# One read-back of the table's rows for both outer blocks, and block 0's norm first on VectorE

## The chip, the cores and the metric

The kernel runs on 1 core of one Trainium2 chip. The metric is device time in microseconds for one execution; lower is better. In the profile PE is TensorE (PEld its weight loads), DVE is VectorE, ACT is ScalarE, POOL is GpSimd, SP is SyncE, which issues the plain DMAs.

## The reference: one graph layer with four relations

There are 625 nodes with 512 features and 20,625 weighted edges of four types (10,000 in both directions and one loop per node), sorted by destination. Each node sums the messages of its edges, is normalized, and goes through a feed-forward network:

```python
h = maximum(layernorm(x), 0)
xs = h[src]
for r in range(4):
    w_r = where(edge_type == r, edge_weight, 0)
    total_msg += (xs @ W_rel[r] + b_rel[r]) * w_r[:, None]
agg = segment_sum(total_msg, dst) / maximum(segment_sum(edge_weight, dst), 1)[:, None]
x1 = layer_norm(h + h @ W_self + b_self + agg, ln1_g, ln1_b)
ffn = gelu(x1 @ W_ffn1 + b_ffn1) @ W_ffn2 + b_ffn2
out = x + layer_norm(x1 + ffn, ln2_g, ln2_b)
```

## The kernel before: a table of messages, then sums by block

The 625 nodes lie in five blocks of 128 rows. The kernel has two parts.

*The rows.* TensorE computes h @ W_rel[r] for each relation and block (`table_rows`, L403): 20 chunks of 128 rows with 512 floats. Each is scaled and biased on VectorE (L416) and stored to a table in device memory by SP (L418). Chunks 15 to 19 stay on the chip in tiles of their own (`m`), and chunks 9 to 14 stay in the three buffers `tr` that hold two chunks each (`held`). Chunks 0 to 8 are only in device memory.

*The sums.* Two ways are in use. For blocks 0 and 4 (`OUTER`), most of the edges whose destinations lie in that one block are put into a matrix of weights from all 2560 table rows to the block's 128 nodes (`sums_w`; block 0's is read from device memory, block 4's is read and then added to by the products of L613 with copies on VectorE and ScalarE, L556 to L566). A sum is then 20 products, one for each chunk (`chunk_sum`, L1302). All other edges go by gathers: GpSimd fetches 128 table rows with one indirect DMA (`gather`, L1159), 99 times, and six more for edges at the start of the inner blocks (`gather_first`, L1216), into ten buffers `ms` in turn. A unit of three gathers is added up: the first scaled on ScalarE (`first_row`, L1165), the others added on VectorE (`row_added`, L1183), then for most units split in a high and a low part (L1169 on ScalarE, L1173 on VectorE), and one or two products on TensorE bring it to the nodes (`edge_sum`, L1205 to L1208). A buffer `ms` comes free when its row has been used.

Each block's sums are added into `z` (`accumulate`, L429, which takes the block's own product, `self_part`, L441, too). Then comes the first norm (`first_norm`: statistics L880, mean L331, root steps L862 to L869, centred L887, scaled L892, bias L896), the turn of its rows by TensorE (L351) with a copy by ScalarE (L1363), the feed-forward (up L928, gelu L932, down L946), the second norm (sum L956, statistics L959, centred L966, scaled L971) and the store by SP (L997). The blocks go through the feed-forward in the order 0, 4, 1, 2, 3. Block 3 is the last, and its norm takes a power on GpSimd (L344) for the root steps.

*What sets the order.* The instructions of the second part are put in order by a planner (`Plan`). Each operation is named with its engine, an estimated duration, what it comes after, the buffers that it takes and gives back, and a rank; `level` replaces the first number of the rank. The planner runs through time and lets each engine take the ready operation with the lowest key. The result is a fixed order for each engine. On the chip an engine waits at an instruction that is not ready, with all that stand behind it. `LAND` and `LATE` are the planner's estimates for the landing of a gather.

Before the change, block 0's sum takes the resident chunks first and then chunks 0 to 8, for which SP reads the table back (`chunk_load`, L1297, five loads, each as soon as one of the three buffers `tr` is free). Block 4's sum follows and starts with chunks 0 to 14, all read back again (eight loads). Both use one accumulator (`one`), so block 4's sum starts when block 0's is in `z`.

## Time and profile before

| what | value |
|---|---|
| median of 3 runs | 260.74 us (260.15 to 263.15) |
| the profiled execution, its time | 262.26 us |
| its span, first to last instruction | 260.5 us |
| mean granted TensorE clock | 0.993 |
| busy: PE, PEld, DVE, ACT, POOL | 246.4, 141.4, 200.5, 74.8, 172.0 us |
| loads of the table by SP (L1297) | 13: 11 of 512 KB, 2 of 256 KB |
| gathers (L1159, L1216) | 99 and 6 |

A row of a timeline gives start, length, engine, line, operation, and in brackets how long the engine had been idle before it and what ended that. A row can merge several instructions (xN). A 128x512 product in f32 shows as two entries. Busy time is what the engine spent in instructions; it doesn't tell whether the end depended on them. TensorE's lengths overlap, as products are pipelined: the distance from one start to the next is the pace.

### The profile page before, as it was taken

The page shows a single profiled execution, that of the slowest core. Times are in us where ns is not written, and L with a number is a line of the kernel's source. Part 1 is how long each engine was busy: PE and PEld are TensorE (multiplying, and loading weights), DVE is VectorE, ACT ScalarE, POOL GpSimd, SP SyncE. Part 2 cuts the span into 40 slices and gives each one's busy share as a digit, 9 for nine tenths or more (in the row PEclk, how much of TensorE's full clock was granted, in tenths as well). Part 3 has the DMA queues.
Part 4 walks back from the last instruction along what each step waited for, and adds up shares of the span by engine and source line. Part 5 has one row for each costly group of instructions (what it writes and reads, how often), then busy time and mean ns, then how long its engine had stood idle before and what let it go on. Part 6 is the DMA issues. An engine that isn't in the chain of part 4 may idle for free. (4 is left out here: it accounts for less than half of the span.)

```text
span 260.5 us, 3515 instructions
## 1 busy us (share of the span) xinstructions
PE 246.4 (95%) x1051; PEld 141.4 (54%) x1051; DVE 200.5 (77%) x503; ACT 74.8 (29%) x224; POOL 172.0 (66%) x230
## 2 busy tenths in 40 slices
PE   8899999999999969999959999989999998899996
PEld 6444444445445625443424444864685964675964
DVE  2896999997979964839879399997798985973614
ACT  3017300000031573623121142641223632310420
POOL 4478889887888577777778777777777777100000
PEclk9999999999999999999999999999999999799999
DMA  5999999972272599799997977777776677330101
GB/s 191 361 402 416 379 382 360 321 285 81 73 253 85 199 363 328 227 346 299 367 325 219 374 232 201 218 191 208 213 212 205 199 204 213 111 110 6 44 0 44
DMA packets 24055, 60.20 MB, mean 231 GB/s; under 512 B 4401, under 2 KB 8753, under 8 KB 22882
## 3 DMA queue, kind: packets, MB, share of 16 engines
q0 software_dynamic: 9936, 27.58, 35.0%
q1 hardware_dynamic: 13808, 30.94, 32.1%
q10 hardware_dynamic: 290, 1.44, 1.6%
q8 instruction: 9, 0.15, 0.2%
q14 instruction: 12, 0.10, 0.1%
HBM read 50.77 MB, written 9.17 MB: 230 GB/s over the span
## 5 line engine op out<-in xcount | busy, mean ns | idle before, releaser
L1159 POOL DMA_INDIRECT ms<-table,row_i x99 | 97.2, 982 | 30.8 <-issue 13.4
L403 PE MATMUL ps<-wr,hT 128*128 128x512 f32 (+2 forms) x168 | 71.2, 576 | 0.0
L686 POOL DMA_INDIRECT cells<-weight,cell x45 | 48.6, 1080 | 9.0 <-issue 6.4
L403 PEld LDWEIGHTS ps<-wr,hT 128*128 128x128 f32 x168 | 30.6, 190 | 33.8 <-issue 29.9
L1183 DVE SCALAR_TENSOR_TENSOR add<-ms,wgt_g,add 128x512 f32<-128x512 f32 x48 | 35.7, 748 | 16.8 <-DMA ms<-table,row_i 14.9
L928 PEld LDWEIGHTS ps<-x1T,w_sb 128*128 128x128 f32 x320 | 39.1, 197 | 5.2 <-issue 3.2
L928 PE MATMUL ps<-x1T,w_sb 128*128 128x128 f32 (+1 forms) x320 | 39.7, 281 | 0.9 <-ACT gT L932 0.9
L1165 ACT ACTIVATE add<-ms,ed 128x512 f32<-128x512 f32 x30 | 20.7, 692 | 66.5 <-DMA ms<-table,row_i 47.3
L946 PE MATMUL ps<-w_sb,gT 128*128 128x512 f32 (+3 forms) x96 | 36.2, 522 | 0.0
L1302 PE MATMUL acc<-tr,sums_w 128*128 128x512 f32 x60 | 27.7, 595 | 0.0
L599 ACT ACTIVATE ohw<-os,w 128x128 fp32r<-128x128 f32 x36 | 11.4, 389 | 56.3 <-DVE os L581 55.3
L946 PEld LDWEIGHTS ps<-w_sb,gT 128*128 128x128 f32 (+1 forms) x96 | 16.6, 188 | 14.4 <-issue 11.8
L932 ACT ACTIVATE gT<-ps,bf 128x128 f32<-128x128 f32 (+1 forms) x40 | 13.3, 362 | 19.6 <-PE ps L928 14.9
L441 PE MATMUL ps<-ws_sb,hT 128*128 128x512 f32 x40 | 18.3, 592 | 0.0
L1302 PEld LDWEIGHTS acc<-tr,sums_w 128*128 128x128 f32 x60 | 11.0, 190 | 12.3 <-issue 11.2
L1208 PE MATMUL acc<-es,oh 128*128 128x512 f32 x24 | 12.9, 626 | 3.2 <-DVE es L1183 3.2
L416 DVE SCALAR_TENSOR_TENSOR tr<-ps,rx,brel_bc 128x512 f32<-128x512 f32 x15 | 11.2, 744 | 3.3 <-POOL idle L689 2.1
L1173 DVE TENSOR_TENSOR el<-add,eh 128x512 fp32r<-128x512 f32 x18 | 12.3, 681 | 0.9 <-ACT eh L1169 0.8
L1169 ACT CAST eh<-add 128x512 fp32r<-128x512 f32 x18 | 10.5, 581 | 8.2 <-DVE add L1183 8.2
L956 DVE TENSOR_TENSOR ow<-ps,z 128x512 f32<-128x512 f32 (+3 forms) x6 | 3.6, 599 | 11.4 <-PE ps L946 11.3
L441 PEld LDWEIGHTS ps<-ws_sb,hT 128*128 128x128 f32 x40 | 7.6, 190 | 8.7 <-issue 8.6
L1205 PE MATMUL acc<-eh,oh 128*128 128x512 f32 x18 | 11.7, 651 | 0.0
(215 smaller groups left out, 302.5 us busy)
## 6 DMA issues: line engine op xcount, KB each, us to landing
tr<-table SPq DMA_DIRECT2D x11, 512.0 KB, 6.3
w_sb<-in_L_gnn_W_ffn_dram SPq DMA_DIRECT2D x2, 2048.0 KB, 9.5
table<-tr SPq DMA_DIRECT2D x15, 256.0 KB, 6.3
wr<-in_L_gnn_W_rel_dram SPq DMA_DIRECT2D x3, 1024.0 KB, 8.8
cells<-zeros SPq DMA_DIRECT2D x2, 1280.0 KB, 12.5
ms<-table,row_i POOLq DMA_INDIRECT x99, 3.8
rows<-in_rows_dram SPq DMA_DIRECT2D x1, 1536.0 KB, 13.0
sums_w<-cells ACTq DMA_DIRECT2D x1, 1280.0 KB, 5.9
```

Source lines behind the costliest of these rows:

```text
L403: nc.tensor.matmul(p_[:, :h.stop - h.start], hT[i][:, k, :], wr_sb[r][:, k, h], start=(k == 0), stop=(k == KD - 1))
L441: nc.tensor.matmul(p[0], hT[i][:, k, :], ws_sb[:, k, :], start=(k == 0), stop=(k == KD - 1))
L686: s = nc.gpsimd.indirect_dma_start(out=cells[i][:, :], out_offset=bass.IndirectOffsetOnAxis(ap=cell[i][:, k:k + 1], axis=0), in_=weight[i] ...
L928: nc.tensor.matmul(pu[:, :nn], w1_sb[:, k, f * P:(f + 1) * P], x1T_b()[:, k, :nn], start=(k == 0), stop=(k == KD - 1))
L932: nc.scalar.activation(box["gT"][:, f, :nn], pus[f][:, :nn], AF.Gelu, bias=bf1[:, f:f + 1])
L946: nc.tensor.matmul(po[h][:n, :w], box["gT"][:, f, at], w2_sb[:, f, c], start=(f == 0), stop=(f == KF - 1))
L1159: nc.gpsimd.indirect_dma_start(out=ms[j], out_offset=None, in_=table[:, :], in_offset=bass.IndirectOffsetOnAxis(ap=row_i[:, j:j + 1], axis=0))
L1165: nc.scalar.activation(box["sum"], ms[j], AF.Copy, scale=wgt[:, j:j + 1])
L1173: nc.vector.tensor_sub(box["low"], box["sum"], box["high"].bitcast(F32))
L1183: nc.vector.scalar_tensor_tensor(to, ms[j], wgt_g[:, k, q - 1:q], box["sum"], op0=ALU.mult, op1=ALU.add)
L1208: nc.tensor.matmul(acc[bs], ohs[0][:, q, :].bitcast(F32), box["sum"] if "sum" in box else ms[j], start=(k == 0), stop=last)
L1302: nc.tensor.matmul(acc[b,], sums_w[b][:, c, :], kept[(b, c) if (b, c) in kept else c], start=first, stop=last)
```

## The change: one load for both blocks, and other ranks

Both outer blocks now use the same copy of a chunk. `turns` gives the order of the 40 products: block 0's resident chunks, then block 4's sum with chunks 9 to 14, then for each load of chunks 0 to 8 block 0's products and block 4's, then block 4's with chunks 15 to 19. A buffer `tr` is given back by block 4's product, as that is the second to use it. So there are five loads instead of thirteen, and the first waits until block 4's weights are complete (`banked`). As both sums are open at once, block 4's has one of the four general accumulators (`ps`) instead of `one`. The own products of blocks 0 and 4 get `level` 1.4, which puts them ahead of the chunk products (1.5). Block 0's addition to `z` and its first norm without the bias get `level` -1, ahead of all else on VectorE. The planner's estimates for a gather's landing are changed. No computation is added or left out.

```diff
@@ -410,7 +410,7 @@
                 kept["pair"] = const.tile([P, CH, D], F32, tag="tr", name=f"tr_{c}", bufs=LA)
             m = kept["pair"][:, k, :]
             if c in held:
-                kept[OUTER[0], c] = m
+                kept[c] = m
         row0 = r * NP + i * P
         for p_, h in zip(p, at):
             made_row.append(nc.vector.scalar_tensor_tensor(m[:, h], p_[:, :h.stop - h.start], rx[:, i, 1:2],
@@ -1008,12 +1008,12 @@
     SUM = 3
     WARM = 24
     ES = 7
-    LAND, LATE = 3.6, ((8, 2.0), (40, 1.2))
+    LAND, LATE = 3.6, ((8, 2.5), (40, 0.5))
     HOTS_AT, SELF_AT, ADDS_AT = (15, 16, 17), 15, (16, 17, 18)
     OHS = 3
     OW = 5
     GT = 2
-    GATHER = 1.26
+    GATHER, LOADED = 1.26, 6.2
     SLACK = 1.2
     LATER = 0.3
     PARTED = 1, 1
@@ -1146,8 +1146,9 @@
     for n, b in enumerate((OUTER[0], OUTER[1], *inner)):
         first, second, added = self_part(b)
         rank = (2, 0.1 * n) if n < len(OUTER) else (5, n)
-        s0 = op("PE", 1.735, first, take=["ps"], rank=rank)
-        s = op("PE", 1.735, second, after=[s0], give=["T"], lag=0.25, rank=rank)
+        level = 1.4 if n < len(OUTER) else None
+        s0 = op("PE", 1.735, first, take=["ps"], rank=rank, level=level)
+        s = op("PE", 1.735, second, after=[s0], give=["T"], lag=0.25, rank=rank, level=level)
         own[b] = op("DVE", 0.68, added, after=[s], give=[("ps", s0)], rank=(0.6,) if b in OUTER else None, level=4.5)
 
     acc = {}
@@ -1291,15 +1292,15 @@
                    after=[m, first_ready], give=["acc"] if b == bs[-1] else [], rank=(0.3, n), level=1.5 if len(bs) == 1 else 0.05)
             adds[b].append(m)
 
-    def chunk_load(b, c, n):
-        t = const.tile([P, CH, D], F32, tag="tr", name=f"tr_{b}_{c}", bufs=LA)
-        kept.update({(b, c + k): t[:, k, :] for k in range(n)})
+    def chunk_load(c, n):
+        t = const.tile([P, CH, D], F32, tag="tr", name=f"tr_again_{c}", bufs=LA)
+        kept.update({c + k: t[:, k, :] for k in range(n)})
         nc.sync.dma_start(t[:, :n, :], table[c * P:(c + n) * P, :].rearrange("(k p) d -> p k d", p=P))
 
     def chunk_sum(b, c, first, last):
         if first:
-            acc[b,] = ps_one.tile([P, D], F32, tag="one", name=f"acc{b}")
-        nc.tensor.matmul(acc[b,], sums_w[b][:, c, :], kept[(b, c) if (b, c) in kept else c], start=first, stop=last)
+            acc[b,] = ps_one.tile([P, D], F32, tag="one", name=f"acc{b}") if b == OUTER[0] else buffer("ps")
+        nc.tensor.matmul(acc[b,], sums_w[b][:, c, :], kept[c], start=first, stop=last)
 
     landed = op("cells", CELLS, None)
     banked, before_ = [op("SP", 0.3, lambda: load_sums(1), after=[landed], lag=6.5, rank=(0, -1))], None
@@ -1331,19 +1332,22 @@
                        after=[before_, *banked[-1:]], rank=(0.5, i), level=0.25)
                 banked.append(op("ACT", 1.05, lambda steps=steps: steps["c"](), after=[e], give=[("ps", bank_op)], rank=(2, i), level=4.5))
 
-    m, ld, t, here = {b: None for b in OUTER}, None, None, {}
+    m, ld, t, here, first_of = {b: None for b in OUTER}, None, None, {}, {}
     stay = range(NL, NC)
-    for i, (b, c) in enumerate([(OUTER[0], c) for c in (NC - 2, *held, *stay[:-2], NC - 1, *range(held[0]))]
-                               + [(OUTER[1], c) for c in (*range(NL), *stay)]):
-        if (b, c) not in here and c < NL and (b, c) not in kept:
+    loaded = [range(c, min(c + CH - (c + NL) % CH, held[0])) for c in range(held[0]) if c == 0 or (c + NL) % CH == 0]
+    turns = [(OUTER[0], c) for c in (NC - 2, *held, *stay[:-2], NC - 1)] + [(OUTER[1], c) for c in held] \
+        + [(b, c) for some in loaded for b in OUTER for c in some] + [(OUTER[1], c) for c in stay]
+    for i, (b, c) in enumerate(turns):
+        if c < held[0] and c not in here:
             n = CH - (c + NL) % CH
-            ld = op("SP", 0.3, lambda b=b, c=c, n=n: chunk_load(b, c, n), after=[ld], take=["tr"], lag=6.2, order=True,
-                    rank=(0, i))
-            here.update({(b, c + k): ld for k in range(n)})
-        first, last = m[b] is None, i % NC == NC - 1
+            ld = op("SP", 0.3, lambda c=c, n=n: chunk_load(c, n), after=[ld], take=["tr"], lag=LOADED, order=True, rank=(0, i))
+            here.update({c + k: ld for k in range(n)})
+        first, last = m[b] is None, (b, c) == [t_ for t_ in turns if t_[0] == b][-1]
         m[b] = op("PE", 0.87, lambda b=b, c=c, first=first, last=last: chunk_sum(b, c, first, last),
-                  after=[m[b], here.get((b, c)), *(banked if b == OUTER[1] else [])], take=["one"] if first else [],
-                  give=["tr"] if c < NL and (c + NL) % CH == CH - 1 else [], lag=0.25, rank=(2, 2 + 0.01 * i), level=1.5)
+                  after=[m[b], here.get(c), *(banked if b == OUTER[1] else [])],
+                  take=[("one", "ps")[OUTER.index(b)]] if first else [],
+                  give=["tr"] if c < NL and b == OUTER[1] and (c + NL) % CH == CH - 1 else [], lag=0.25, rank=(2, 2 + 0.01 * i), level=1.5)
+        first_of.setdefault(b, m[b])
         if i == 8:
             t = op("PE", 0.2, lambda: at_.update(copied=total_outside()), after=[m[b], first_ready], take=["ps"], lag=8.0, rank=(2, 2.085))
             t = op("DVE", 0.15, lambda: at_["copied"](), after=[t], give=[("ps", t)], lag=2.0, rank=(0.5,), level=4.5)
@@ -1351,7 +1355,8 @@
             op("PE", 0.1, read_outside, after=[t, m[b]], rank=(2, 2.365))
     for b in OUTER:
         adds[b].append(op("DVE", 0.72, lambda b=b: add_to(b, lambda: acc[b,], slice(0, P)),
-                          after=[m[b], first_ready], give=["one"], rank=(0.4,)))
+                          after=[m[b], first_ready], give=["one" if b == OUTER[0] else ("ps", first_of[b])], rank=(0.4,),
+                          level=-1 if b == OUTER[0] else None))
 
     turned = {}
     sums_done = {}
@@ -1371,7 +1376,8 @@
             made[name] = op(eng, us, fn, after=[made[a] for a in needs] if needs else dep + [own[b]],
                             lag=1.0 if name == "x1" and b != inner[-1] else 0.08, take=["ow"] if name in ("a", "x1") else [],
                             give=[("ow", made["a"])] if name == "x1" else [],
-                            rank=(0.4,) if b in OUTER and name != "bias" else None)
+                            rank=(0.4,) if b in OUTER and name != "bias" else None,
+                            level=-1 if b == OUTER[0] and name != "bias" else None)
         p = {}
         parts_ = ((0, KD // 2), (KD // 2, KD)) if b == inner[-1] else ((0, KD),)
         for k0, k1 in parts_:
```

SP, behind the loads of weights and the table's stores (`tr_4_9` is block 4's own read of chunks 9 and 10, `tr_again_1` the common read of chunks 1 and 2); the numbers at the ends of names count tiles:

```order
-L1297 DMA tr_4_9_1315<-table_152 128x2x512
-L1297 DMA tr_4_11_1322<-table_152 128x2x512
-L1297 DMA tr_4_13_1330<-table_152 128x2x512
+L706 DMA sums_w4_980<-cells_4_100 128x2560
+L1298 DMA tr_again_0_1201<-table_152 128x512
+L1298 DMA tr_again_1_1211<-table_152 128x2x512
+L1298 DMA tr_again_3_1229<-table_152 128x2x512
+L1298 DMA tr_again_5_1262<-table_152 128x2x512
+L1298 DMA tr_again_7_1277<-table_152 128x2x512
 L1143 TENSOR_LOAD n_out_157
```

Ten of the thirteen old loads stand above this piece; block 4's weights (L706) are read ahead of all loads in both orders.

TensorE at the last sums of gathered rows (L1208 before, L1209 now; `es_124` is the last unit of three, the next row a single gather), with block 2's feed-forward around them and block 3's turn (L351). Before:

```order
L1208 MATMUL acc3_1_1701<-es_124_1891,oh_122_1844 128x512
L1208 MATMUL acc3_1_1701<-ms_8_951,oh_125_1874 128x512
L928 MATMUL ps_1_79<-x1T_2_1752,w1_sb_93 128x128 x4
L928 MATMUL ps_0_78<-x1T_2_1752,w1_sb_93 128x128 x4
L928 MATMUL ps_3_81<-x1T_2_1752,w1_sb_93 128x128 x4
L946 MATMUL ps_2_80<-w2_sb_94,gT_2_1855 128x512 x4
L351 MATMUL ps_1_79<-ident_120,ow_0_953 128x128 x2
L351 MATMUL ps_0_78<-ident_120,ow_0_953 128x128 x2
L946 MATMUL ps_2_80<-w2_sb_94,gT_2_1855 128x512 x4
L928 MATMUL ps_3_81<-x1T_3_1955,w1_sb_93 128x128 x4
```

Now:

```order
L1209 MATMUL acc3_1_1675<-es_124_1871,oh_122_1824 128x512
L1209 MATMUL acc3_1_1675<-ms_3_946,oh_125_1853 128x512
L928 MATMUL ps_1_79<-x1T_2_1775,w1_sb_93 128x128 x4
L928 MATMUL ps_0_78<-x1T_2_1775,w1_sb_93 128x128 x4
L946 MATMUL ps_3_81<-w2_sb_94,gT_2_1826 128x512 x6
L351 MATMUL ps_2_80<-ident_120,ow_0_953 128x128 x2
L351 MATMUL ps_1_79<-ident_120,ow_0_953 128x128 x2
L946 MATMUL ps_3_81<-w2_sb_94,gT_2_1826 128x512 x2
L928 MATMUL ps_0_78<-x1T_3_1938,w1_sb_93 128x128 x4
```

Behind the last sum there are two up-projections instead of three, and behind the turn two down products instead of four; three up-projections stand between the unit before and this one in both orders.

VectorE on the way to block 3's norm (`acc3_1` is its last sum, L880 the statistics, L966 and L971 the second norms of blocks 0, 4 and 1). Before:

```order
L966 SCALAR_TENSOR_TENSOR ow_1_954<-ow_4_957,mv_y1_0_1887,rows_89 128x512
L868 SCALAR_TENSOR_TENSOR rs_y1_0_1889<-rs_y1_0_1889 128x1
L869 SCALAR_TENSOR_TENSOR rs_y1_0_1889<-rs_y1_0_1889 128x1
L971 SCALAR_TENSOR_TENSOR ow_0_953<-ow_2_955,rs_y4_0_1791,xs_87 128x512
L868 SCALAR_TENSOR_TENSOR rs_y1_0_1889<-rs_y1_0_1889 128x1
L869 SCALAR_TENSOR_TENSOR rs_y1_0_1889<-rs_y1_0_1889 128x1
L429 SCALAR_TENSOR_TENSOR z_145<-acc3_1_1701,rdeg_179,z_145 128x512
L971 SCALAR_TENSOR_TENSOR ow_4_957<-ow_1_954,rs_y1_0_1889,xs_87 128x512
L880 BN_STATS st_z3_1932<-z_145 128x6
```

Now:

```order
L971 SCALAR_TENSOR_TENSOR ow_2_955<-ow_1_954,rs_y0_0_1652,xs_87 128x512
L971 SCALAR_TENSOR_TENSOR ow_0_953<-ow_3_956,rs_y4_0_1793,xs_87 128x512
L429 SCALAR_TENSOR_TENSOR z_145<-acc3_1_1675,rdeg_179,z_145 128x512
L966 SCALAR_TENSOR_TENSOR ow_2_955<-ow_4_957,mv_y1_0_1863,rows_89 128x512
L880 BN_STATS st_z3_1914<-z_145 128x6
L971 SCALAR_TENSOR_TENSOR ow_4_957<-ow_2_955,rs_y1_0_1865,xs_87 128x512
L331 BN_AGGR mv_z3_1921<-st_z3_1914 128x2
L334 TENSOR_SCALAR rs_z3_1923<-mv_z3_1921 128x1
L887 SCALAR_TENSOR_TENSOR ow_1_954<-z_145,mv_z3_1921,rows_89 128x512
```

The addition of the last sum (L429) now stands ahead of block 1's centring (L966), which writes the buffer that block 0's output is stored from, and the scaled outputs of blocks 0 and 4 stand right ahead of it.

Block 0's addition and norm, which stood among the row additions of units 50 to 58, now stand among those of units 65 to 75, directly behind block 0's last chunk product.

## The prediction

> **What bounds the kernel now.** I read the table of groups first, then GpSimd's rows in order of time, the waits of TensorE from the end of the rows on, the busy time of four stretches, and last the timeline of TensorE and VectorE over the last 40 us.
>
> GpSimd in order of time (start, length, idle before), the first two gathers, one in the middle, the last two; above them the two groups that count them (count, sum, mean ns):
>
> ```profile
> L1159 POOL DMA_INDIRECT ms<-table,row_i x99 | 97.2, 982 | 30.8 <-issue 13.4
> L1216 POOL DMA_INDIRECT ms<-table,x_row x6 | 5.7, 945 | 1.8 <-DMA ms<-table,row_i 0.9 <-issue 0.6 <-DVE rs_z L868 0.3
> ...
> 88.09 1.10 POOL L1159 DMA_INDIRECT ms<-table,row_i  x1 [0.94 <-DVE od L591]
> 89.50 1.01 POOL L1159 DMA_INDIRECT ms<-table,row_i  x1 [0.30 <-issue]
> ...
> 136.39 2.37 POOL L1159 DMA_INDIRECT ms<-table,row_i  x1 [0.30 <-DVE z L429]
> ...
> 220.47 0.94 POOL L1159 DMA_INDIRECT ms<-table,row_i  x1 [0.30 <-issue]
> 221.72 0.94 POOL L1159 DMA_INDIRECT ms<-table,row_i  x1 [0.30 <-DVE add L1183]
> ```
>
> 105 gathers stand in 134.6 us, 1.28 us each: 0.95 of issue and 0.30 of fixed gap. The gap stays 0.30 where a releaser is named, so no gather ever waits for a buffer. From 88 to 222.7 us GpSimd's issuing sets the pace. One issue took 2.37 us, 1.42 more than the usual 0.95.
>
> Busy time by stretch (length, then PE, PEld, DVE, ACT, POOL, clock, DMA share, GB/s), and the two large waits of TensorE before 220 us (start, length, idle before):
>
> ```profile
> 88.00:142.00 54.00, 48.43 (x146) 22.93 (x145) 39.14 (x89) 21.57 (x47) 41.42 (x42) 1.00 0.91 311
> 142.00:153.00 11.00, 11.00 (x27) 4.93 (x26) 6.43 (x10) 1.90 (x3) 8.26 (x10) 1.00 0.93 329
> 153.00:182.00 29.00, 27.39 (x122) 17.38 (x121) 27.20 (x59) 11.73 (x23) 22.28 (x23) 1.00 0.72 204
> 182.00:222.00 40.00, 38.30 (x203) 26.40 (x201) 32.58 (x74) 14.78 (x33) 30.27 (x32) 1.00 0.72 208
> 222.00:227.10 5.10, 4.66 (x18) 3.61 (x19) 4.93 (x13) 1.60 (x4) 0.66 (x1) 0.67 0.40 116
> ...
> 94.57 1.10 PE L1208 MATMUL acc<-ms,oh 128*128 128x512 f32 x2 [1.82 <-issue]
> ...
> 136.73 1.12 PE L1208 MATMUL acc<-es,oh 128*128 128x512 f32 x2 [3.03 <-DVE es L1183]
> ```
>
> TensorE is almost full too, but its large waits stand before sums of gathered rows (L1208 takes them, or what VectorE made of them; the third, 1.74 us, is in the next fence). DMA is at 0.91 to 0.93 while the table is read back and at 0.72 with gathers alone.
>
> TensorE at the end (start, length; a 128x128 or 128x512 f32 product is two of its entries):
>
> ```profile
> 222.28 0.49 PE L1206 MATMUL acc<-el,oh 128*128 128x512 f32 x1 [1.74 <-DVE el L1173]
> 222.93 1.52 PE L1208 MATMUL acc<-es,oh 128*128 128x512 f32 x2 [0.16 <-DVE es L1183]
> 224.24 4.13 PE L928 MATMUL ps<-x1T,w_sb 128*128 128x128 f32 x24
> ...
> 229.07 1.02 PE L1208 MATMUL acc<-ms,oh 128*128 128x512 f32 x2
> 229.93 2.84 PE L928 MATMUL ps<-x1T,w_sb 128*128 128x128 f32 x24
> 232.61 3.60 PE L946 MATMUL ps<-w_sb,gT 128*128 128x512 f32 x8
> 236.05 0.60 PE L351 MATMUL ps<-ident,ow 128*128 128x128 f32 x4
> 236.48 3.60 PE L946 MATMUL ps<-w_sb,gT 128*128 128x512 f32 x8
> 239.92 7.31 PE L928 MATMUL ps<-x1T,w_sb 128*128 128x128 f32 x64
> 247.06 7.11 PE L946 MATMUL ps<-w_sb,gT 128*128 128x384 f32 x32
> ```
>
> After the last sum (229.07) block 2's feed-forward fills TensorE; at 236.05 block 3's normalized rows are turned; four more products of block 2 (236.48 to 239.92) stand ahead of block 3's feed-forward, which then runs to 254. VectorE on the same stretch:
>
> ```profile
> 220.87 0.75 DVE L1183 SCALAR_TENSOR_TENSOR add<-ms,wgt_g,add 128x512 f32<-128x512 f32 x1 [2.47 <-DMA ms<-table,row_i]
> 225.71 0.74 DVE L1183 SCALAR_TENSOR_TENSOR es<-ms,wgt_g,add 128x512 f32<-128x512 f32 x1
> 229.50 0.75 DVE L966 SCALAR_TENSOR_TENSOR ow<-ow,mv_y,rows 128x512 f32<-128x512 f32 x1 [1.82 <-DMA out_dram<-ow]
> 231.48 0.74 DVE L429 SCALAR_TENSOR_TENSOR z<-acc,rdeg,z 128x512 f32<-128x512 f32 x1
> 235.02 0.88 DVE L892 SCALAR_TENSOR_TENSOR ow<-ow,rs_z,rows 128x256 f32<-128x256 f32 x2 [0.47 <-POOL rs_z L344]
> ```
>
> The turn at 236.05 follows VectorE's last step of the norm (235.02 to 235.90), whose chain started at 231.48. So the end is: gathers (GpSimd), then VectorE's chain to the turn, then TensorE's filler, then 14.1 us of TensorE and the last norm and store.
>
> **The change part by part.**
>
> *The eight loads that go.* Issues to landing, from the table of DMA issues:
>
> ```profile
> tr<-table SPq DMA_DIRECT2D x11, 512.0 KB, 6.3
> ...
> tr<-table SPq DMA_DIRECT2D x2, 256.0 KB, 6.2
> ```
>
> Thirteen loads of 6.1 MB become five of 2.3 MB (4 x 512 and 256 KB); SP has no other work there. As GpSimd is bound by issuing, 3.8 MB less on the DMA engines is worth nothing by itself: none of TensorE's large waits is for a load. It can be worth the long issue at 136.39, which stands in the crowded stretch. Between 0 and -1.42 us. I take -0.4, nearer to none, as 104 other issues in the same or a lighter load were no such thing and the median run is 1.5 us below the profiled one, so it may not have the long issue at all.
>
> *The sums over the table, and their order.* TensorE does the same 40 products. Blocks 0 and 4's own products (4 x 0.43 x 2 = 3.4 us each) move ahead of them. Block 0's sum ends much later, block 4's a little earlier. TensorE's waits of 1.82 us (ahead of 94.57) and 3.03 us (ahead of 136.73) should mostly go, since the gathers then land among fewer loads and TensorE has other sums to do. I cost this at nothing: TensorE then reaches the later sums sooner and waits there instead, since the gathers come no earlier. If that cover were gone, the gain would be up to 4.8 us; it shows only if the last gathers are also early, so I leave it out of the sum.
>
> *The wait that is added.* Block 4's sum with resident rows now releases the buffers for the loads, and VectorE's z addition of block 0 waits for the last load's product. Behind it on VectorE stand the row additions that free GpSimd's ten gather buffers. The last copy of block 4's weights is now
>
> ```profile
> 109.12 0.44 ACT L566 COPY sums_w<-sum 128x140 f32<-128x140 f32 x1
> ```
>
> By hand: they are ready near 112 us, as two casts now stand ahead on ScalarE; TensorE gets to them near 114, releases buffers at 116 to 121, the loads land 6.3 us later each, the third and fourth after a second release near 131 and 135, the last near 142; block 0's sum ends at 144 to 146. VectorE gets to the addition near 148, since the row additions ahead of it need gathers issued up to 142. Cost 0, with 2 to 4 us to spare.
>
> *Block 0's norm in front on VectorE.* It now runs near 125 to 137 us:
>
> ```profile
> 122.58 0.75 DVE L429 SCALAR_TENSOR_TENSOR z<-acc,rdeg,z 128x512 f32<-128x512 f32 x1
> ...
> 130.77 0.74 DVE L892 SCALAR_TENSOR_TENSOR ow<-ow,rs_z,rows 128x512 f32<-128x512 f32 x1
> ...
> 137.26 0.68 DVE L896 TENSOR_TENSOR z<-ow,rows 128x512 f32<-128x512 f32 x1
> ...
> 163.56 1.95 PE L928 MATMUL ps<-x1T,w_sb 128*128 128x128 f32 x16
> ```
>
> Its first use is at 163.56, so it was 30 us early. It moves to about 148 to 157 us: five full-width steps of 0.7 and some twelve small ones of 0.15 to 0.21, about 5.7 us of VectorE. The stretches 142 to 153 and 153 to 182 have 4.6 and 1.8 us of idle VectorE, 6.4 in all: it fits, but VectorE is then full there, and 7.4 us of idle time from 182 to 222 absorb what is late. Cost between 0 and the part of 5.7 that exceeds the buffers' slack (below); I take 0.
>
> *The tail.* In the new order two products of block 2 instead of four stand between the turn and block 3, and two up-projections instead of three behind the last sum. Against that, VectorE has a 0.28 us mask and a 0.33 us pair of root steps behind its wait at 220.87, so the last row addition comes 0.6 later (226.9). Then 0.25 and six pairs of about 0.35, two scaled outputs of 0.66, the z addition at 230.6 to 231.2, the step L966 that waits for the store of the first of these (2.2 us from 229.9 as now, so 232.1 to 232.8), the statistics, 0.65 for another output, and the rest of the chain as now (1.3 and 0.9): the turn at 236.65, 0.6 later. TensorE gets there before: the last sum ends near 229.0, then 2 x 0.89 and 6 x 0.86 make 236.0. Then 0.44 and 2 x 0.86: block 3's feed-forward starts at 238.8, not 239.92: -1.1. Bounds: +0.6 if the filler saved buys nothing, and -2.6 if also the gather behind the wait at 220.87 lands in 3.7 us, as others do:
>
> ```profile
> 211.73 3.71 DMA ms<-table,row_i
> ...
> 215.48 5.30 DMA ms<-table,row_i
> ```
>
> *The clock.* In 222 to 227.1 us the granted clock was 0.67, after TensorE's wait of 1.74 us; 24 entries took 4.13 us where the next 24 took 2.84. The wait of 3.03 us before 136.73 left it at 1.00 (first stretch). This cost nothing at the end, as VectorE's chain ended last. A cold stretch that now falls between the last sum and the turn would take 1.3 us, of which the spare 0.6 (236.0 against 236.65) is free and 0.7 shows. [...]
>
> Sum: -0.4 - 1.1 = -1.5 us on the profiled span of 260.5, 259.0. The profiled execution took 262.26 us in all, the three runs shown 260.15 to 263.15 with a median of 260.74. I put the difference on the median: **259.2 us**. A measurement of this kernel can tell about 1% from no change, 2.6 us, so this is "no change".
>
> **The rivals.**
> - *The extras go with the loads (faster).* One of the long issue (1.42) and the late landing (5.30 - 3.71 = 1.6) goes besides the tail's 1.1: 258.1; both: 256.6. Taken together 257.4. For it: DMA was at 0.93 and falls to about 0.72 from 142 us on. Against: the late landing at 215 us lies long after the last load.
> - *The change doesn't move the end.* VectorE's chain to the turn slips as much as TensorE's filler shrinks (the clock, or the store that L966 waits for): 260.7. For it: the tail's gain is 1.1 us out of a chain of 16 us that I only worked by hand.
> - *VectorE stands before block 0's sum (slower).* If the loads come late, VectorE waits at the z addition, row additions queue behind it, and a gather waits for its buffer. A buffer is used again ten gathers later, 12.8 us after the first issue; the latest release now is this row's, 7.9 us after its issue at 165.46, ending at 174.07, with the next issue of that buffer at 178.4 at the earliest:
>
> ```profile
> 173.34 0.73 DVE L1183 SCALAR_TENSOR_TENSOR es<-ms,wgt_g,add 128x512 f32<-128x512 f32 x1
> ...
> 165.46 0.95 POOL L1159 DMA_INDIRECT ms<-table,row_i  x1 [0.30 <-issue]
> ```
>
> So 4.3 us of lateness are free and every one beyond them moves the end by one. It decides when block 0's sum ends later than about 152 us; to be slower by 1% it must end near 156, which is 10 us after my working. Then the time is 260.7 - 1.1 + 3.9 = 263.5. Against it: a load lands in 6.3 us now under a fuller DMA.
>
> **How the numbers follow.** Forecast 0.45 (258.1 to 260.2), faster rival 0.25 (257.4), no move 0.18 (260.7), slower rival 0.12 (263.5). Below 258.1 lie the 0.25 and 0.02 of the forecast: faster 0.27. Slower 0.12, all of the slower rival. Same 0.61. The range runs from 256.8, which leaves out the case with both extras gone and an even better tail, to 263.0, short of most of the slower rival.
>
> **What would show it.** Right: 105 gathers with gaps of 0.30 and the last issue at 221 to 223 us; five loads between 115 and 145; block 0's z addition near 148 with little wait before it; the turn of block 3 near 236.6 and its feed-forward two products later. Wrong: a gap above 0.30 ahead of a gather (the slower rival); the last issue at 221.5 or earlier (the faster one); the turn after 237.5, or a clock below 1 after 226 us (no move).

## The result and the profile after

The changed kernel takes 259.8 us (median of 21 runs), the kernel before 261.8 us (21 runs beside them). By the ratio, 0.9945 with a 95% interval of 0.9924 to 0.9966, that is 1.4 us less (0.9 to 2.0); the two medians are 2.0 us apart. The forecast was 1.5 us less, and "no change" by the bound of 1%. A later series on one chip gave 259.29 against 260.76 us, ratio 0.9949 (0.9915 to 0.9983). The profile below is of that series (its execution took 259.25 us, span 257.5). One execution of the changed kernel took 420 us at a granted clock of 0.56, and beside eight later runs the kernel before took 311 to 317 us; neither is compared here.

TensorE at the end of the changed kernel (start, length, idle before; two entries are one product), answering to the rows that end at 247.06 before:

```profile
221.61 0.50 PE L1207 MATMUL acc<-el,oh 128*128 128x512 f32 x1 [0.43 <-DVE el L1174]
221.94 1.02 PE L1209 MATMUL acc<-es,oh 128*128 128x512 f32 x2
222.80 2.84 PE L928 MATMUL ps<-x1T,w_sb 128*128 128x128 f32 x24
...
226.34 1.02 PE L1209 MATMUL acc<-ms,oh 128*128 128x512 f32 x2
227.19 1.95 PE L928 MATMUL ps<-x1T,w_sb 128*128 128x128 f32 x16
228.98 5.32 PE L946 MATMUL ps<-w_sb,gT 128*128 128x512 f32 x12
234.24 0.90 PE L351 MATMUL ps<-ident,ow 128*128 128x128 f32 x4
234.97 1.88 PE L946 MATMUL ps<-w_sb,gT 128*128 128x512 f32 x4
236.69 7.31 PE L928 MATMUL ps<-x1T,w_sb 128*128 128x128 f32 x64
```

The last sum stands at 226.34 (229.07 before), the turn of block 3 at 234.24 (236.05), its feed-forward at 236.69 (239.92). The profiled span is 3.0 us shorter, more than the medians are apart.

GpSimd's first and last gather and the longest issue:

```profile
86.62 0.98 POOL L1160 DMA_INDIRECT ms<-table,row_i  x1 [1.27 <-DVE xw L820]
...
177.64 1.77 POOL L1160 DMA_INDIRECT ms<-table,row_i  x1 [0.30 <-issue]
...
221.18 0.95 POOL L1160 DMA_INDIRECT ms<-table,row_i  x1 [0.30 <-DVE es L1184]
```

Ahead of every gather but the first stands a gap of 0.30 us (0.31 at most), as before. The first is 1.47 us earlier, the last only 0.54. So the 3.0 us of the two profiles split, in order of time, into: first gather 1.47 earlier; gathers 0.93 slower; last gather to last sum 2.19 less (7.35 to 5.16); last sum to feed-forward 0.50 less (10.85 to 10.35); feed-forward to the end 0.23 more (20.58 to 20.81).

The read-back and block 0's norm: the loads in the table of issues and on SP's queue, the last products of block 0's sum on TensorE, then the z addition and the last scaling on VectorE:

```profile
tr_again<-table SPq DMA_DIRECT2D x4, 512.0 KB, 5.4
...
tr_again<-table SPq DMA_DIRECT2D x1, 256.0 KB, 4.0
```

```profile
116.86 19.39 SPq L1298 DMA_DIRECT2D tr_again<-table  x5
```

```profile
144.29 1.88 PE L1303 MATMUL acc<-tr_again,sums_w 128*128 128x512 f32 x4
```

```profile
146.73 0.73 DVE L429 SCALAR_TENSOR_TENSOR z<-acc,rdeg,z 128x512 f32<-128x512 f32 x1
...
154.00 0.74 DVE L892 SCALAR_TENSOR_TENSOR ow<-ow,rs_z,rows 128x512 f32<-128x512 f32 x1
```

Five loads are issued from 116.9 to 136.3 us, block 0's sum ends at 146.2, and VectorE comes to the z addition 0.6 us later, with no wait in the row.

Busy time by stretch, as before (PE, PEld, DVE, ACT, POOL, clock, DMA share, GB/s):

```profile
88.00:142.00 54.00, 49.83 (x148) 23.94 (x147) 35.37 (x71) 21.48 (x49) 41.21 (x43) 1.00 0.82 268
142.00:153.00 11.00, 11.00 (x28) 5.03 (x27) 9.81 (x21) 3.17 (x5) 8.26 (x10) 1.00 0.72 209
153.00:182.00 29.00, 26.48 (x117) 16.40 (x116) 25.15 (x57) 10.52 (x21) 22.51 (x22) 0.96 0.69 199
182.00:222.00 40.00, 39.15 (x216) 28.07 (x215) 34.69 (x75) 16.14 (x36) 30.65 (x31) 0.99 0.71 204
222.00:227.10 5.10, 5.10 (x31) 3.76 (x30) 4.86 (x20) 1.93 (x7) 0.13 (x1) 1.00 0.30 93
```

DMA falls from 0.91 and 0.93 to 0.82 and 0.72 in the first two stretches, and GpSimd's pace does not change with it (41.21 us busy against 41.42, 8.26 against 8.26). TensorE is busy 1.4 us longer in the first stretch, 0.9 less in the third, and without a hole from 222 on. Its waits have moved:

```profile
110.04 0.47 PE L1206 MATMUL acc<-eh,oh 128*128 128x512 f32 x1 [1.74 <-DVE z L429]
...
129.59 1.12 PE L1209 MATMUL acc<-es,oh 128*128 128x512 f32 x2 [2.04 <-DVE es L1184]
...
177.98 1.13 PE L1209 MATMUL acc<-es,oh 128*128 128x512 f32 x2 [2.50 <-DVE es L1184]
```

### The profile page after: what moved, and what is told of

Read it like the earlier page. It is cut to its first block, busy times and chain, and to the rows that moved or that the text cites. A ratio compares the mean times of both kernels' runs of the same rounds, so it can differ in the third digit from the quotient of the medians.

```text
span 418.3 us, 3507 instructions
## 1 busy us (share of the span) xinstructions
PE 415.6 (99%) x1051; PEld 190.0 (45%) x1051; DVE 200.8 (48%) x501; ACT 76.5 (18%) x224; POOL 167.2 (40%) x230
## 4 chain that ended last, share of the span: by engine, by line
PE 99%; issue 0%; DVE 0%
PE ps L403 30%; PE ps L946 15%; PE ps L928 15%; PE acc L1209 8%; PE ps L1303 7%; PE ps L441 7%; PE acc L1303 7%; PE ps L351 2%; PE ps L613 2%; PE acc L1207 2%; PE acc L1206 2%; PE spin L1227 1%; PE warm L1053 1%; PE add L786 1%; PE ps L798 0%; PE add L784 0%
## 5 line engine op out<-in xcount | busy, mean ns | idle before, releaser
L403 PE MATMUL ps<-wr,hT 128*128 128x512 f32 (+2 forms) x168 | 125.3, 931 | 0.0
L403 PEld LDWEIGHTS ps<-wr,hT 128*128 128x128 f32 x168 | 37.6, 230 | 75.1 <-issue 72.0
L928 PEld LDWEIGHTS ps<-x1T,w_sb 128*128 128x128 f32 x320 | 62.9, 279 | 10.2 <-issue 8.8
L928 PE MATMUL ps<-x1T,w_sb 128*128 128x128 f32 (+1 forms) x320 | 64.0, 383 | 0.0
L946 PE MATMUL ps<-w_sb,gT 128*128 128x512 f32 (+3 forms) x96 | 63.4, 840 | 0.0
L946 PEld LDWEIGHTS ps<-w_sb,gT 128*128 128x128 f32 (+1 forms) x96 | 21.1, 237 | 33.6 <-issue 32.0
L441 PE MATMUL ps<-ws_sb,hT 128*128 128x512 f32 x40 | 32.2, 965 | 0.0
L429 DVE SCALAR_TENSOR_TENSOR z<-acc,rdeg,z 64x512 f32<-64x512 f32 (+1 forms) x9 | 6.8, 750 | 47.4 <-PE acc L1209 46.6
L1209 PE MATMUL acc<-es,oh 128*128 128x512 f32 x24 | 20.6, 966 | 0.0
L1303 PE MATMUL acc<-tr_again,sums_w 128*128 128x512 f32 x18 | 15.1, 967 | 0.0
L1303 PE MATMUL ps<-tr_again,sums_w 128*128 128x512 f32 x18 | 15.1, 967 | 0.0
```

The lines of the kernel that those rows point to most:

```text
L403: nc.tensor.matmul(p_[:, :h.stop - h.start], hT[i][:, k, :], wr_sb[r][:, k, h], start=(k == 0), stop=(k == KD - 1))
L441: nc.tensor.matmul(p[0], hT[i][:, k, :], ws_sb[:, k, :], start=(k == 0), stop=(k == KD - 1))
L928: nc.tensor.matmul(pu[:, :nn], w1_sb[:, k, f * P:(f + 1) * P], x1T_b()[:, k, :nn], start=(k == 0), stop=(k == KD - 1))
L946: nc.tensor.matmul(po[h][:n, :w], box["gT"][:, f, at], w2_sb[:, f, c], start=(f == 0), stop=(f == KF - 1))
L1209: nc.tensor.matmul(acc[bs], ohs[0][:, q, :].bitcast(F32), box["sum"] if "sum" in box else ms[j], start=(k == 0), stop=last)
L1303: nc.tensor.matmul(acc[b,], sums_w[b][:, c, :], kept[c], start=first, stop=last)
```

## The experiments

The theory was that GpSimd's gather issues set the pace and that the gain is made between block 3's turn and its feed-forward. Rival 1 was the loads that went, rival 2 TensorE's total work with its waits.

**The changed kernel again.** No edit.

> The changed kernel once more, on a further chip. Theory (GpSimd's gather issues set the pace, the gain is made between the turn of block 3 and its feed-forward): ratio near 0.9945, 105 gathers with gaps of 0.30 us, the last issue at 221 to 223 us, the turn near 236.6 us, the feed-forward two products later at 238.8 us. Rival 1 (the loads that went): no issue longer than about 1.1 us, the last issue at 221.5 us or earlier, turn and feed-forward earlier by the same. Rival 2 (TensorE's total work): its waits before 222 us are 3 to 5 us less in sum, and the last sum is ready by as much earlier. Where the kernel before takes over 300 us again, the run tells none of them apart.

Ratio 0.9949. Last issue, gaps and ratio came as the theory has them; turn and feed-forward came 2.4 and 2.1 us earlier than it said. Of rival 1's signs, the last issue at 221.5 us or earlier is there (221.18), inside the theory's own range; the other is not: there are issues up to 1.77 us, and what issues take beyond 0.95 us (those over 1.0) adds up to 4.4 us, against 3.5 before. Rival 2's sign is there at less than half its size: TensorE is idle for 7.5 us between 86 and 222 us, against 8.9 before. TensorE from 86 us to the start of block 3's feed-forward, before and after (length, then PE busy):

```profile
86.00:239.92 153.92, 144.61 (x578) 84.39 (x576) 119.30 (x265) 54.91 (x120) 104.22 (x107) 0.99 0.74 234
```

```profile
86.00:236.69 150.69, 143.10 (x580) 83.83 (x579) 118.43 (x263) 55.09 (x120) 104.83 (x106) 0.99 0.70 213
```

TensorE is idle for 9.31 us before and 7.59 after; busy time is 1.5 us less for the same products.

**The one line on landings, in the kernel before.** All thirteen loads stay, and block 0's norm stays early. The table is the planner's estimate of how much later than its 3.6 us the first gathers land.

```diff
-    LAND, LATE = 3.6, ((8, 2.0), (40, 1.2))
+    LAND, LATE = 3.6, ((8, 2.5), (40, 0.5))
```

> The kernel before with the changed kernel's table of late landings alone: all thirteen loads stay and block 0's norm stays early, but two products instead of four stand between the turn of block 3 and its feed-forward. Theory (the gain is made there): 1.1 us are gained by this line alone, ratio 0.996. Rival 1 (the loads that went, by the gathers' landings and long issues): 1.000. Rival 2 (TensorE's total work sets the end): 1.000.

259.92 against 261.98 us, ratio 0.9926 (0.9891 to 0.9961). The line alone gains about as much as the whole change, with every load in place, so the loads aren't needed for a gain of this size: 1.000, the number of rival 1 and of rival 2, is out. GpSimd's last gather and TensorE in the profile:

```profile
220.99 0.94 POOL L1159 DMA_INDIRECT ms<-table,row_i  x1 [0.30 <-issue]
```

```profile
223.80 1.16 PE L928 MATMUL ps<-x1T,w_sb 128*128 128x128 f32 x8 [2.54 <-DVE ow L956]
...
229.07 1.02 PE L1208 MATMUL acc<-ms,oh 128*128 128x512 f32 x2
229.93 1.95 PE L928 MATMUL ps<-x1T,w_sb 128*128 128x128 f32 x16
231.71 5.32 PE L946 MATMUL ps<-w_sb,gT 128*128 128x512 f32 x12
236.87 0.60 PE L351 MATMUL ps<-ident,ow 128*128 128x128 f32 x4
...
239.02 7.31 PE L928 MATMUL ps<-x1T,w_sb 128*128 128x128 f32 x64
```

```profile
86.00:239.02 153.02, 145.22 (x575) 84.68 (x574) 120.53 (x265) 54.87 (x120) 102.82 (x107) 0.98 0.74 236
```

Two products do stand ahead of the turn instead of behind it, but TensorE is busy from the last sum to the feed-forward, here as before. Moving work within a full stretch wins nothing here: the turn itself is 0.82 us later than in the kernel before. What is won from the last sum on, 0.9 us (9.95 against 10.85), is one group of up-projections that now stands ahead of the last sum; that sum comes at 229.07 in both. Idle is 7.80 us instead of 9.31. This profiled execution took 261.45 us, 1.5 above its median: TensorE's wait of 2.54 us hangs on a gather that took 7.11 us to land (the table in the next section), and a slow clock follows it (granted 0.95 from 216 to 226 us and 0.88 from 226 to 236).

**The former line on landings, in the changed kernel.** Five loads; the former table.

```diff
-    LAND, LATE = 3.6, ((8, 2.5), (40, 0.5))
+    LAND, LATE = 3.6, ((8, 2.0), (40, 1.2))
```

> The changed kernel with the former table of late landings: five loads as in the changed kernel, but no product at all between the turn of block 3 and its feed-forward. In the changed kernel's undisturbed profile the turn is at 234.24 us and the feed-forward at 236.69, with two products (1.7 us) between. Theory: the turn stays where VectorE's norm puts it, the feed-forward follows it by 0.5 to 0.7 us, 1.7 us earlier: ratio to the kernel before 0.988. Rival 1 (loads): 0.9945, as the changed kernel. Rival 2 (TensorE's total work): 0.9945, since TensorE's fill only moves to another place and its waits with it.

259.11 against 261.98 us, ratio 0.9887 (0.9840 to 0.9935), as the theory's number has it, and 0.9945 lies outside. Its profile:

```profile
227.58 1.02 PE L1209 MATMUL acc<-ms,oh 128*128 128x512 f32 x2
228.44 5.31 PE L946 MATMUL ps<-w_sb,gT 128*128 128x512 f32 x12
233.59 0.60 PE L351 MATMUL ps<-ident,ow 128*128 128x128 f32 x4
234.03 0.71 PE L1227 MATMUL spin<-zeros 128*128 128x256 bf16 x5
234.57 7.31 PE L928 MATMUL ps<-x1T,w_sb 128*128 128x128 f32 x64
```

```profile
86.00:234.57 148.57, 143.10 (x586) 84.23 (x586) 119.74 (x266) 54.67 (x120) 104.43 (x106) 1.00 0.71 216
```

The feed-forward starts 5.35 us earlier than before and 2.12 earlier than in the changed kernel; idle is 5.47 us. VectorE's last piece of the norm ended at 232.5, so TensorE's fill (block 2's products ahead of the turn), not VectorE's chain, sets the turn. The number was met, the mechanism only in part: the theory had the turn stay at 234.24 and the distance from it to the feed-forward shrink by 1.7 us, and the profile has the turn 0.65 earlier and the distance 1.47 shorter. The profiled execution did not keep those 2.12 us, because its last stores landed late. The two last stores (median us to landing), in this kernel and in the changed one:

```profile
out_dram<-ow SPq DMA_DIRECT2D x1, 160.0 KB, 4.2
out_dram<-ow SPq DMA_DIRECT2D x1, 96.0 KB, 4.0
```

```profile
out_dram<-ow SPq DMA_DIRECT2D x1, 160.0 KB, 2.1
out_dram<-ow SPq DMA_DIRECT2D x1, 96.0 KB, 1.9
```

By the medians this version is the best of the full kernels. That it beats the changed one is likely and not settled: the intervals of the ratios (up to 0.9935, from 0.9924) overlap, and they come from two series. It does show that the rest of the change (loads, order of the sums, the norm's place) needs no help from the line: it gains 1.1% without it. Each half alone gains (0.7% and 1.1%), and both together no more (0.55%), so the gains of the two don't add up.

**Six gathers left out.** The changed kernel without the issues for two units of block 2's edges. Everything that follows them on the other engines stays.

```diff
         ms[j] = buffer("ms")
+        if j in left_out:
+            return
         nc.gpsimd.indirect_dma_start(
...
+        left_out.extend(j for u in (units[3:5] if bs == (2,) else []) for j in u)
```

> The changed kernel with six of the 99 gathers of edge rows left out (two units of block 2's own edges: their row additions, casts and products stay and use what stands in the buffers, so the output is not the reference's). Order and work of all other engines are the same. Theory (GpSimd's issues set the pace): 6 x 1.25 = 7.5 us less until the last gather, of which TensorE gives back what it has to wait for no more; its waits between 86 and 222 us are 7.5 us in sum in the changed kernel, so the end comes 5 to 7.5 us earlier: ratio to the kernel before 0.967 to 0.976. Rival (VectorE or TensorE sets the pace and the gathers merely keep up): under 1 us, ratio 0.991 to 0.9945.

255.57 against 261.98 us, ratio 0.9763 (0.9717 to 0.9809): 6.2 us less than before and 4 to 5 less than the changed kernel (4.1 by the profiles, 1.9% by the ratios), at the lower edge of the theory. The rival that the gathers merely keep up is out. The last gather, a gather that waited in the middle, and TensorE:

```profile
153.58 0.94 POOL L1162 DMA_INDIRECT ms<-table,row_i  x1 [1.16 <-DVE rs_z L868]
...
215.57 1.00 POOL L1162 DMA_INDIRECT ms<-table,row_i  x1 [0.30 <-issue]
```

```profile
86.00:232.47 146.47, 140.99 (x579) 83.05 (x578) 117.88 (x263) 55.65 (x120) 98.54 (x100) 1.00 0.70 208
```

The last gather is 5.61 us earlier, not 7.5, since five gathers between 149 and 163 us now wait 0.65 to 1.16 us. In part the edit itself makes these waits: the first of them, at 149.88, is the first gather behind the six, and its buffer, one of ten in turn, was filled only four gathers earlier (144.42), 5.5 us before, where ten gathers take 12.9 us in the changed kernel. The norm of block 0 and the next one stand between the row additions on VectorE there, too, so how much of the waits is the slower rival's mechanism stays open. The feed-forward comes 4.22 us earlier: the gather behind TensorE's last wait is issued 5.68 us earlier, but takes 5.82 us to land, against 4.26.

**Seven earlier runs of these kernels.** Same edits as above: the changed kernel (three times), the former line in it (twice), the line alone (twice). Beside them the kernel before took 311 to 317 us, so a step of 1 to 2 us can't be read from them.

> The changed kernel once more, for undisturbed records. Theory (GpSimd's gather issues set the pace, the gain is made between the turn of block 3 and its feed-forward): 105 gathers with gaps of 0.30 us and the last issue at 221 to 223 us, the turn near 236.6 us, block 3's feed-forward two products later at 238.8 us, ratio near 0.9945. Rival 1 (the loads that went): no issue longer than about 1.1 us, the last issue at 221.5 us or earlier and turn and feed-forward earlier by the same. Rival 2 (TensorE's total work sets the end): its waits before 222 us are 3 to 5 us less in sum and the last sum is ready by as much earlier.

313.59 us; the kernel before 311.47. No ratio of use.

> The changed kernel with the former table of late landings (2.0 us for the first 8 gathers, 1.2 us up to the 40th). The loads are five as in the changed kernel, but now no product at all stands between the turn of block 3 and its feed-forward (before: four, changed: two), and six down-projections alone stand behind the last sum. Theory: the turn stays near 236.6 us, the feed-forward starts at 237.1 us, 2.8 us earlier than before: ratio 0.989, 1.7 us better than the changed kernel. Rival 1 (loads) and rival 2 (TensorE's total): as the changed kernel, ratio 0.9945.

310.74 against 311.47 us.

> The kernel before with the changed kernel's table of late landings alone (2.5 us for the first 8 gathers, 0.5 us up to the 40th): all thirteen loads stay, block 0's norm stays early, but two products instead of four stand between the turn of block 3 and its feed-forward. Theory: the tail's 1.1 us are gained with this line alone, ratio 0.996. Rival 1 (loads): 1.000. Rival 2 (TensorE's total): 1.000.

312.20 against 311.47 us.

> The changed kernel again, on another chip: on the last one the kernel before took 311.5 us, not 261.8, and the granted clock was 0.91 in the changed kernel, so its records say nothing on the steps. Theory (GpSimd's gather issues set the pace, the gain is made between the turn of block 3 and its feed-forward): 105 gathers with gaps of 0.30 us, the last issue at 221 to 223 us, the turn near 236.6 us, the feed-forward two products later at 238.8 us; ratio near 0.9945. Rival 1 (the loads that went): no issue longer than about 1.1 us, the last issue at 221.5 us or earlier, turn and feed-forward earlier by the same. Rival 2 (TensorE's total work): its waits before 222 us are 3 to 5 us less in sum and the last sum is ready by as much earlier.

312.84 against 312.44 us, ratio 1.0032 (0.9955 to 1.0108).

> The changed kernel with the former table of late landings, again. No product stands between the turn of block 3 and its feed-forward (before: four, changed: two); six down-projections alone stand behind the last sum. Theory: turn near 236.6 us, feed-forward at 237.1, 2.8 us earlier than before: ratio 0.989, 1.7 us better than the changed kernel, if the sums themselves are no later. Rival 1 (loads) and rival 2 (TensorE's total): as the changed kernel, ratio 0.9945.

312.36 against 312.44 us.

> The changed kernel once more: on the two chips asked so far the kernel before took 311 to 312 us instead of 262, so what they say of steps of one microsecond is nothing. Theory (GpSimd's gather issues set the pace, the gain is made between the turn of block 3 and its feed-forward): ratio near 0.9945, 105 gathers with gaps of 0.30 us, the last issue at 221 to 223 us, the turn near 236.6 us, the feed-forward two products later at 238.8 us. Rival 1 (the loads that went): no issue longer than about 1.1 us, the last issue at 221.5 us or earlier, turn and feed-forward earlier by the same. Rival 2 (TensorE's total work): its waits before 222 us are 3 to 5 us less in sum, and the last sum is ready by as much earlier.

317.86 against 317.32 us, ratio 1.0113 (1.0032 to 1.0193), the one interval that lies above 1; why is open.

> The kernel before with the changed kernel's table of late landings alone: all thirteen loads stay, block 0's norm stays early, but two products instead of four stand between the turn of block 3 and its feed-forward. Theory: the 1.1 us of the tail are gained by this line alone, ratio 0.996. Rival 1 (loads): 1.000. Rival 2 (TensorE's total): 1.000.

318.24 against 317.32 us, ratio 0.9991 (0.9923 to 1.0059).

**Block 0's norm without its front place.** The changed kernel without `level=-1`, in both places; four products then stand between turn and feed-forward, as before the change.

```diff
-                          after=[m[b], first_ready], give=["one" if b == OUTER[0] else ("ps", first_of[b])], rank=(0.4,),
-                          level=-1 if b == OUTER[0] else None))
+                          after=[m[b], first_ready], give=["one" if b == OUTER[0] else ("ps", first_of[b])], rank=(0.4,)))
...
-                            rank=(0.4,) if b in OUTER and name != "bias" else None,
-                            level=-1 if b == OUTER[0] and name != "bias" else None)
+                            rank=(0.4,) if b in OUTER and name != "bias" else None)
```

> The changed kernel without the front place of block 0's norm on VectorE. Loads are five as in the changed kernel; four products stand between the turn of block 3 and its feed-forward, as before the change. Theory: the feed-forward starts at 240.5 us if the turn stays near 236.6, or at 240 with the turn of before; with at most 0.4 us from the loads the ratio is 0.9985 to 1.002. Rival 1 (loads): 0.9945, as the changed kernel. Rival 2: 0.9945.

311.70 us; the kernel before took 311.47 beside it, so this can't be read either, and it was not run again. What the front place is worth by itself stays open.

## Why the prediction was right, and where its steps were not

The size was right (1.5 forecast; 1.4 measured, 0.9 to 2.0), and GpSimd's pace was read rightly: a gather that goes moves the end by 0.7 to 0.8 us (4 to 5 us for six), and no gather waits for a buffer in the kernel before or in the changed one. The last issue at 221.2 lay in the range given for the forecast, but also where I had put the faster rival's sign, so that sign told nothing. The sum, though, was made of the wrong terms, and that it met the measured size is luck.

The chain of each profile, followed back from block 3's feed-forward, runs through TensorE, which has no hole above 0.16 us there, to a wait of TensorE (1.74, 0.43, 2.54, 0.32 and 1.10 us in the order of the table below). From the end of that wait it goes through VectorE to the landing of one gather, and to that gather's issue. In the changed kernel the gather and the row addition that waits for it are:

```profile
214.56 4.26 DMA ms<-table,row_i
```

```profile
218.91 0.76 DVE L1184 SCALAR_TENSOR_TENSOR add<-ms,wgt_g,add 128x512 f32<-128x512 f32 x1 [1.62 <-DMA ms<-table,row_i]
```

The same four pieces in all five profiles, in us:

| kernel | that gather's issue | issue to landing | landing to the end of TensorE's wait | from there to block 3's feed-forward | its start |
|---|---|---|---|---|---|
| before | 215.48 | 5.30 | 1.50 | 17.64 | 239.92 |
| changed | 214.56 | 4.26 | 2.79 | 15.08 | 236.69 |
| the line alone | 214.73 | 7.11 | 1.96 | 15.22 | 239.02 |
| former line | 212.18 | 4.69 | 2.02 | 15.68 | 234.57 |
| six gathers left out | 208.88 | 5.82 | 2.69 | 15.08 | 232.47 |

So the 3.23 us by which the feed-forward is earlier in the changed kernel are 0.92 of issue and 1.04 of landing, less 1.29 on VectorE, plus 2.56 on TensorE behind its last wait. 1.70 of these 2.56 are a stretch at a granted clock of down to 0.50 that no longer falls there (with the line alone, 1.7 of the 15.22 are one: 0.05 and 0.12 of 10 us each).

- *The loads, -0.4.* Not found, and not excluded. Thirteen loads with the new line give 0.9926, five give 0.9945 and 0.9949, each interval holding the other value; but 0.4 us is 0.15%, less than these intervals can tell, and what the loads have of the 1.1% that the change gains without the line was not separated. Long issues stand in all five profiles (sums of 2.2 to 4.4 us beyond 0.95) and are no fewer where the loads are gone, so the faster rival's 1.4 us has no support. Its late landing did shrink, by 1.04 of 1.6 us. Landings in the table go from 5.30 and 7.11 us with thirteen loads to 4.26, 4.69 and 5.82 with five, one execution each and some 70 us after the last load is issued, so whether the loads have a part in it stays open.
- *TensorE's waits, 0.* "TensorE then reaches the later sums sooner and waits there instead" holds: waits of 1.74, 2.04 and 2.50 us stand at new places, and the last wait ends with a gather in all five profiles. Up to the feed-forward TensorE is idle for 1.72 us less than before, but the idle sum alone doesn't set the time: it is 5.47 us in the kernel at 259.11 us and 5.48 in the one at 255.57.
- *The tail, -1.1.* This is the step that did not hold. It took the landing behind VectorE's wait (220.87 before) as unchanged, had the turn held by VectorE and 0.6 us later, and the distance from the turn to the feed-forward 1.7 us shorter. Measured: that wait ended at 218.91, the last row addition came 1.34 us earlier instead of 0.6 later, and VectorE's last step of the norm ended at 234.58 instead of 235.90. The turn came 1.81 us earlier, with TensorE's fill ending at the same time, and the distance was 1.42 shorter. That distance is no gain in itself: from the last sum to the feed-forward TensorE has no hole above 0.05 us in any of the five profiles (with the former line, products on zeros, L1227, fill 0.5 us), so moving products from behind the turn to ahead of it wins nothing there. What is won on this stretch, 0.50 us in the changed kernel and 0.90 with the line alone, is the group of up-projections that left it.
- *The added wait and the norm, 0.* Right: loads between 116.9 and 136.3, block 0's sum at 146.2 (144 to 146 forecast), the z addition at 146.7 (148), VectorE 9.81 of 11 us busy from 142 to 153. The slower rival needed the sum 6 us later.
- *The clock, 0 to 0.7.* "This cost nothing at the end" nearly holds for the profile that it was read from: VectorE's norm ended at 235.90 and TensorE's fill at 236.21, so 0.3 us at most. It isn't so in general: with the line alone they end at 234.56 and 237.03, and the slow stretch shows in full. In the changed kernel the stretch stands after the wait of 2.50 us at 178, and TensorE still waits for 0.43 us behind it, at 221.61, so it costs the end nothing there. Before (two stretches of 10 us) and after:

```profile
216.00:226.00 10.00, 8.05 (x36) 5.38 (x35) 7.32 (x19) 2.44 (x5) 5.14 (x6) 0.88 0.66 187
226.00:236.00 10.00, 10.00 (x53) 7.13 (x53) 7.47 (x21) 1.99 (x6) 1.01 (x1) 0.95 0.21 76
```

```profile
176.00:186.00 10.00, 8.02 (x22) 4.05 (x23) 9.78 (x20) 1.75 (x3) 8.12 (x7) 0.83 0.62 178
```

Read by the microsecond, the granted clock before is 0.77, 0.50, 0.50 and 0.53 from 223 to 227 us: 1.70 us of work less than at 1.00. After, 0.17 of 10 us are 1.7 us too: the 8 entries of L946 from 178.94 take 5.29 us there, where the 8 from 236.48 before take 3.60. Why a wait is followed by such a stretch, or isn't, no run shows.

The profiles are one execution each, where the 21 runs of the kernel before spread over 3.8 us (259.64 to 263.45), so the terms of the profiles (3.0 us) can't be laid on the medians (1.4) one by one. How much of the 1.4 us is the new order and how much the landings is open.

## What to carry to other kernels

When one engine sets the pace by issuing and another is nearly full, follow the chain back from the last stretch to the full engine's last wait, and add up what stands on it: the issue, the landing, the steps between and the work behind that wait. Moving work within a stretch that has no hole was worth nothing here: with the line alone two products left the place behind the turn, and the turn came 0.82 us later. Where a planner sets the order, try its estimates alone before crediting the data movement that was changed with them: here one line of landing times gained about what the whole change did, and the change without that line gained at least as much.

## What the runs showed that was not expected

Which wait the slow clock follows does not go by its length in these profiles. Behind waits of 1.74 us (ending at 222.28 before), 2.50 (changed kernel), 2.26 and 2.54 (line alone, ending at 95.00 and 223.80) the granted clock fell: to 0.50 by the microsecond before, to 0.83 over 176 to 186 us in the changed kernel, to 0.87 over 96 to 106 and 0.88 over 226 to 236 with the line alone. Behind those of 1.82 and 3.03 us (before) and 1.74 and 2.04 (changed kernel) it was 1.00; the two kernels whose longest waits between 86 us and the feed-forward are 1.30 and 1.75 us (former line, six gathers left out) had clock 1.00 up to there.

The first gather's 1.5 us go with the last store of the table. GpSimd's step ahead of that gather (L701) waits 1.54 us for a store before and not at all in the changed kernel. The store's issue on SP took 0.85 us before and 1.54 with the line alone, but 0.32 in all three profiles of kernels with five loads. Before and after:

```profile
84.39 0.85 SPq L418 DMA_DIRECT2D table<-m  x1
```

```profile
84.30 0.32 SPq L418 DMA_DIRECT2D table<-m  x1
```

The gathers then start at 88.1 and 88.5 us against 86.5 to 86.8. SP's work up to there is the same in all of them; the cause was not tried. By the last gather 0.9 of the 1.5 us had been lost again to longer issues.
